# The first unit of an attention stack: its operand stacks sent by two queues in blocks of 128 queries, and two small computations moved behind the first norm

## The chip, the cores and the metric

The kernel runs on one core of one Trainium2 chip. Its engines are TensorE (PE, with its weight loads listed apart as PEld), VectorE (DVE), ScalarE (ACT), GpSimd (POOL) and SyncE (SP); each runs its own instructions in order, and semaphores order them against one another. SP and ACT also issue DMA transfers, each on a queue of its own. The metric is the device time of one launch in microseconds (us), as a median over runs.

## The reference

The input is x, 8 sequences of 512 tokens with 128 features, in float32. Six attention layers run one after another on the normalized input, and a gated feed-forward block closes:

```python
q = (h @ wq.T + bq_).reshape(bh, sl, H, DH)          # H = 16 heads of DH = 8
k = (h @ wk.T + bk_).reshape(bh, sl, H, DH)
scores = jnp.einsum('blhd,bmhd->bhlm', q, k) * inv_sqrt_d
w_avg = jax.nn.softmax(scores, axis=-1).mean(axis=1)
new_w = jax.nn.softmax(CSCALE * w_avg + rel[None], axis=-1)
sa = jnp.einsum('blm,bme->ble', new_w, h)
h1 = _ln(h + sa, l1w, l1b)
h2 = _ln(h1, l2w, l2b)
ff = jax.nn.relu(h2 @ w1.T + b1_) @ w2.T + b2_
return (_ln(h2 + ff, l3w, l3b), None)
```

The heads' softmax weights are averaged over the 16 heads, a fixed decay is added, and a second softmax mixes the rows of h. All 16 x 512 x 512 scores of a sequence must pass through an exponential in each layer. The result is x plus the stack's output, and then that plus the feed-forward block of its norm.

## The kernel before, in words

A unit is one layer of one sequence: 6 layers x 8 sequences = 48 units (`units`, L202), in that order. A unit's scores are made in 16 groups: four blocks of 128 queries (`lc`) times four strips (`turn`) of four heads. A group is four matmuls into PSUM of 128 x 512, for 32 queries and 4 heads each (`scores`, L376): a reduce on DVE takes the negated row maximum (`peak`, L394), ACT takes the exponential and its row sum (`exps`, L399), POOL makes reciprocal weights (`weights`, L406) and PE gathers the weighted sum over heads into `acc` (`gather`, L417). The exponentials of a group stand in a buffer of the pool `e`, which has four; six PSUM buffers (`ring`) hold scores.

The matmul of a strip contracts over 128 partitions that hold four pieces of 32: key and query are each split into a high part (its upper bits) and a low part (the rest), and the products of the parts are stacked. So keys and queries have to be copied into stacks on other partitions before scores can start:

- `norm_in` and `norm_steps` normalize x into h: statistics on DVE, then four POOL instructions.
- `turn_h` transposes h on PE, and ACT copies the result to hT (L223).
- `project_k` and `project_q` multiply hT by the weights, and ACT adds the bias (L230, L239; the query's is the scaled bias `bqs`, made at L148).
- `split` makes the high part on DVE (L247) and the low part on POOL (L248).
- `stack_k` issues 16 DMA transfers of 64 KB on SP's queue (L263): four quarters of the partitions (high, low, high, low) times four strips, the quarter being the outer loop.
- `mask_q` on POOL (L278) spreads a block's queries over four heads with a mask; `stack_q` then issues 16 transfers of 128 KB on SP (L294), eight of the high and eight of the low part. One call of both halves covers two of the four query blocks; blocks 2 and 3 follow during the unit's first steps.

The order is written by hand. Each unit has 32 steps (PAIRS), two score matmuls each. `at(step, place, fn)` puts a function into a table, and the main loop calls what stands there for PE, DVE and ACT after a step's score matmuls, maxima and so on. `place` is the point of the step at which the functions are called, not the engine on which they issue: masks and stacks stand at DVE's place, and issue on POOL and SP. `plan_before` (L501) puts a unit's norm two units ahead of it, its projections, splits and stacks of the first half one unit ahead (steps s+3 to s+21, with s one unit before its own step t), and the second half at t to t+3. `plan_turns` (L488) puts the transposes of the unit after next at the last step of a unit. For units 0 and 1 these steps lie before the first score matmul; steps -64 to -1 are run through with nothing else in them. So the first 40 us hold this chain alone.

Ahead of it stand the loads: two sequences of x, four loads of layer 0 on SP (`load_layer`, L104, with the sum `b2s` of two bias rows on POOL at L118), nine small columns on ACT (L129), and the scaled bias `bqs` on DVE. `b2s` is read only in `affine_b`, during the next unit. `load_layer` is called again during the fifth sequence of each layer for the next one.

Of the kernel before, what the change touches and what calls it, by code (L numbers as in the profile page):

```python
# [9 lines left out]
F32 = mybir.dt.float32  # L10
# [3 lines left out]
ALU = mybir.AluOpType  # L14
# [3 lines left out]
P = 128  # L18
H = 16
STRIPS = 4  # L20
PER_STRIP = H // STRIPS
QB = 32
# [7 lines left out]
def attn_stack_then_ffn(ctx: ExitStack, tc: tile.TileContext, a: dict, out: bass.AP):  # L30
    nc = tc.nc
    ctx.enter_context(tc.manual_schedule())
    x = a["x"]
    B, L, E = x.shape
# [7 lines left out]
    NB = P // QB  # L42
    ISD = 1.0 / math.sqrt(E // H)
# [3 lines left out]
    wts = ctx.enter_context(tc.tile_pool(name="wts", bufs=1))  # L47
    state = ctx.enter_context(tc.tile_pool(name="state", bufs=1))
    proj = ctx.enter_context(tc.tile_pool(name="proj", bufs=2))
    epool = ctx.enter_context(tc.tile_pool(name="e", bufs=4))  # L50
    work = ctx.enter_context(tc.tile_pool(name="work", bufs=2))
# [50 lines left out]
    lay = {}  # L102

    def load_layer(d):  # L104
        qk = wts.tile([P, 2, E], F32, tag="wqk", name=f"wqk_{d}", bufs=2)
        nc.sync.dma_start(qk, a["wqk"][d].rearrange("t e o -> e t o"))
        w1 = wts.tile([P, F], F32, tag="w1", name=f"w1_{d}", bufs=2)
        nc.sync.dma_start(w1, a["w1t"][d])
        w2 = wts.tile([P, FC, E], F32, tag="w2", name=f"w2_{d}", bufs=2)
        nc.sync.dma_start(w2, a["w2t"][d].rearrange("(c p) e -> p c e", p=P))  # L110
        r = wts.tile([P, len(ROWS), E], F32, tag="rows", name=f"rows_{d}", bufs=2)
        nc.sync.dma_start(
            r.rearrange("p k e -> p (k e)"),
            a["rows"][d].rearrange("k e -> (k e)").partition_broadcast(P),
        )
        rows = {name: r[:, k, :] for k, name in enumerate(ROWS)}
        b2s = wts.tile([P, E], F32, tag="b2s", name=f"b2s_{d}", bufs=2)
        nc.gpsimd.tensor_tensor(b2s, rows["ln2_b"], rows["b2"], ALU.add)  # L118
        rows["b2s"] = b2s
        lay[d] = (qk, w1, w2, rows)  # L120

    cols = {}
# [22 lines left out]
        nc.sync.dma_start(fw3s, a["f_w3s"].partition_broadcast(P))  # L145

    bqs = wts.tile([P, D], F32, name="bqs")
    nc.vector.tensor_scalar_mul(bqs, cols["bq_col"], ISD)  # L148


    acc = ps_fix.tile([P, L], F32, name="acc")
# [4 lines left out]
    def ring(shape, n):  # L156
        return ps_big.tile(shape, F32, tag="big", name=n)
# [46 lines left out]
    PAIRS = LC * STRIPS * 2  # L204

    class Unit:
# [50 lines left out]
        def stack_k(self):  # L257


            self.ks = proj.tile([P, STRIPS, L], F32, tag="ks", name=f"ks_{self.n}")  # L260
            for c in range(4):
                for i in range(STRIPS):
                    nc.sync.dma_start(  # L263
                        self.ks[32 * c : 32 * c + 32, i, :],
                        self.kparts[c % 2][32 * i : 32 * i + 32, :],
                    )

        def mask_q(self, two, k, lc):


            key = two, k
            if lc == 2 * two:
                self.stacks[key] = work.tile(
                    [P, 2, NB, PER_STRIP, QB], F32, tag=f"m{k}", name=f"m{k}_{self.n}_{two}", bufs=1
                )
            m = self.stacks[key]
            part = self.qparts[k][:, lc * P : (lc + 1) * P].rearrange("p (n l) -> p n l", l=QB)
            nc.gpsimd.tensor_tensor(  # L278
                m[:, lc - 2 * two],
                part.unsqueeze(2).to_broadcast([P, NB, PER_STRIP, QB]),  # L280
                mask.unsqueeze(1).to_broadcast([P, NB, PER_STRIP, QB]),
                ALU.mult,
            )

        def stack_q(self, two, k):
# [6 lines left out]
            for c in (2 * k, 2 * k + 1):  # L292
                for i in range(STRIPS):
# [2 lines left out]
                        m[32 * i : 32 * i + 32].rearrange("p a n j l -> p (a n j l)"),  # L296
                    )


        def norm_a(self):  # L300
            self.ln = Norm(self.z1, self.z1, f"a{self.n}")
# [159 lines left out]
    PE_, DVE_, ACT_, RING_ = range(4)  # L461
    later = {}

    def at(step, place, fn):
        later.setdefault((step, place), []).append(fn)
# [10 lines left out]
    def matmuls(step, fn):  # L476

        at(step, PE_, lambda: at(step, ACT_, fn()))

    def norm_steps(base, un, make, s0, s1, s2, s3, s4):  # L480

        at(base + s0, DVE_, lambda: (make(), un.ln.stats(0, 2)))
        at(base + s1, DVE_, lambda: un.ln.stats(2, LC))
        at(base + s2, DVE_, lambda: un.ln.aggregate())
        at(base + s3, DVE_, lambda: un.ln.centre())
        at(base + s4, DVE_, lambda: un.ln.scale())

    def plan_turns(u):  # L488


        def run():
            rest = []
            if 0 <= u + 2 < U:
                rest.append(obj[u + 2].turn_h(ring([P, L], f"pt_h{u + 2}")))
            if 0 <= u - 1 < U:
                rest.append(obj[u - 1].turn_u(ring([P, L], f"pt_u{u - 1}")))
            return lambda: [fn() for fn in rest]

        at(u * PAIRS + PAIRS - 1, RING_, run)

    def plan_before(un):  # L501

        t = un.u * PAIRS
        if un.d == 0:
            norm_steps(t - 2 * PAIRS, un, un.norm_in, 9, 14, 26, 28, 29)
        s = t - PAIRS
        matmuls(s + 3, un.project_k)
        matmuls(s + 5, un.project_q)
        at(s + 5, DVE_, un.split_k)
        at(s + 8, DVE_, un.split_q)  # L510
        at(s + 6, DVE_, un.stack_k)
        for k, lc, step in ((0, 0, 18), (0, 1, 19), (1, 0, 20), (1, 1, 21)):
            at(s + step, DVE_, lambda k=k, lc=lc: un.mask_q(0, k, lc))
            at(t + 2 * k + lc, DVE_, lambda k=k, lc=lc: un.mask_q(1, k, 2 + lc))
        for k, step in ((0, 19), (1, 21)):
            at(s + step, DVE_, lambda k=k: un.stack_q(0, k))
            at(t + 2 * k + 1, DVE_, lambda k=k: un.stack_q(1, k))

    def plan_after(un):

        s = (un.u + 1) * PAIRS
        norm_steps(s, un, un.norm_a, 11, 12, 13, 14, 15)
        at(s + 16, DVE_, lambda: un.affine_a(0))
        at(s + 17, DVE_, lambda: un.affine_a(1))
        norm_steps(s, un, un.norm_b, 19, 20, 22, 23, 24)
        at(s + 25, DVE_, lambda: un.affine_b(0))
        at(s + 26, DVE_, lambda: un.affine_b(1))
        s += PAIRS
        for f, step in enumerate((11, 13, 19, 21)):
            matmuls(s + step, lambda f=f: un.hidden(f))  # L530
        for half, step in enumerate((27, 29)):
            at(s + step, PE_, lambda half=half: un.mlp_out(half))
            at(s + step, DVE_, lambda half=half: un.mlp_add(half))
        norm_steps(s, un, un.norm_c, 28, 30, PAIRS, PAIRS + 9, PAIRS + 10)
        at(s + PAIRS + 11, DVE_, lambda: un.affine_c(0))
        at(s + PAIRS + 12, DVE_, lambda: un.affine_c(1))
# [21 lines left out]
    for s in range(-2 * PAIRS, 0):  # L558
        if s % PAIRS == 0:
            u = s // PAIRS + 2  # L560
# [5 lines left out]
    for u, un in enumerate(obj):  # L566
# [12 lines left out]
        for pr in range(PAIRS):  # L579
            s = u * PAIRS + pr  # L580
            lc, turn, half = pr // 8, (pr // 2) % STRIPS, pr % 2
# [11 lines left out]


    plan_turns(U)
    ready = {}
    left = iter(sorted({s for s, _ in later}))
# [135 lines left out]
```

## Time and profile before

| what | value |
|---|---|
| median of 3 runs | 2818.68 us (2818.52 to 2821.95) |
| profiled execution | 2825.2 us, of it the span of the profile 2823.4 us |
| PE busy | 2746.7 us, 97% of the span |
| ACT busy | 2496.5 us, 88% |
| DVE busy | 2393.9 us, 85% |
| POOL busy | 1801.2 us, 64% |
| 3072 score matmuls, their reduces, their exponentials: mean | 477, 682 and 840 ns |
| first score matmul, first exponential | 39.93 and 41.49 us after the span's start |
| first exponential of group 2 | 47.47 us after the start |

The profile is one execution, taken by the hardware profiler. Busy times are sums of the durations of an engine's instructions, which overlap the instructions beside them, so that a mean of 840 ns goes with starts 0.67 us apart. PE's ends are modelled. In a line of the timeline the figures are start, length, engine, line, operation, output and input with their sizes, how many were merged, and in square brackets how long the engine was idle before, and what ended that. SPq and ACTq are the queues on which SP and ACT issue transfers.

### The profile page before, as it was taken

What the parts mean: (1) busy time and instruction counts of PE and PEld (TensorE: products, weight loads), DVE (VectorE), ACT (ScalarE), POOL (GpSimd) and SP (SyncE); (2) the same over time, 40 slices, a digit from 0 to 9 for tenths busy, and PEclk for the clock granted to TensorE, in tenths of its full rate; (3) what the DMA queues carried; (4) which work ended last, traced back from release to release, by engine and by line L of the source; (5) the groups of instructions that cost most, each with busy time, mean ns of one, the idle gap of its engine ahead of it and who ended that gap; (6) DMA issues with size and microseconds to landing.
All of it is one profiled execution on the core that took longest, in us unless ns stands there. A gap on an engine that the chain in (4) does not pass through costs nothing.

```text
span 2823.4 us, 51628 instructions
## 1 busy us (share of the span) xinstructions
PE 2746.7 (97%) x14944; PEld 1370.0 (49%) x14944; DVE 2393.9 (85%) x5942; ACT 2496.5 (88%) x6845; POOL 1801.2 (64%) x2205
## 2 busy tenths in 40 slices
PE   5999999999999999999999999999999999989999
PEld 2444545445454454454544545445445454445554
DVE  4999999999999999999999999999999999921110
ACT  5999999999999999999999999999999999933232
POOL 4668776776766767767677676676776767633210
PEclk9999999999999999999999999999999999999999
DMA  5555444544544445444454454454564444300000
GB/s 117 114 118 132 93 104 104 112 108 106 111 105 107 97 113 115 110 92 103 105 127 104 93 113 106 103 120 94 117 153 95 102 105 110 78 8 8 15 12 8
DMA packets 133387, 271.06 MB, mean 96 GB/s; under 512 B 39024, under 2 KB 56560, under 8 KB 133104
## 3 DMA queue, kind: packets, MB, share of 16 engines
q1 hardware_dynamic: 131808, 267.73, 42.3%
q8 instruction: 119, 1.95, 0.3%
q14 instruction: 164, 1.34, 0.2%
q10 hardware_dynamic: 1296, 0.03, 0.0%
HBM read 13.86 MB, written 2.10 MB: 6 GB/s over the span
## 4 chain that ended last, share of the span: by engine, by line
PE 47%; ACT 22%; DVE 18%; POOL 6%; issue 5%; DMA 0%; SPq 0%; POOLq 0%; ACTq 0%; DVEq 0%
ACT e L399 19%; DVE top L394 14%; PE ps L385 13%; PE acc L420 12%; PE py L348 6%; PE ph L644 6%; PE po L445 3%; PE pk L229 1%; ACT w L427 1%; POOL z L306 1%; PE pq L238 1%; POOL rs_a L178 1%; POOL z L186 1%; POOL z L181 1%; ACT g L338 1%
## 5 line engine op out<-in xcount | busy, mean ns | idle before, releaser
L399 ACT ACTIVATE e<-ps,top 128x512 f32<-128x512 f32 x3072 | 2134.5, 840 | 23.9 <-DVE top L394 20.4
L394 DVE TENSOR_REDUCE top<-ps 128x1 f32<-128x512 f32 x3072 | 1952.5, 682 | 42.9 <-PE ps L385 35.8
L385 PE MATMUL ps<-ks,qs 128*128 128x512 f32 x3072 | 1240.0, 477 | 34.2 <-ACT e L399 26.0
L399 ACT ACTIVATION_READ_ACCUMULATOR e<-ps,top 128x1 f32 x3072 | 1103.5, 359 | 0.0
L385 PEld LDWEIGHTS ps<-ks,qs 128*128 128x128 f32 x3072 | 495.4, 189 | 888.3 <-ACT e L399 661.6
L420 PE MATMUL acc<-e,rp 128*32 128x512 f32 x6144 | 819.1, 605 | 0.8 <-POOL rp L410 0.3
L410 POOL TENSOR_TENSOR rp<-pick,r 128x128 f32<-128x128 f32 x768 | 308.1, 401 | 549.8 <-DVE r L408 265.8
L420 PEld LDWEIGHTS acc<-e,rp 128*32 128x32 f32 x6144 | 121.0, 108 | 263.1 <-issue 126.5
L278 POOL TENSOR_TENSOR m<-hiq,mask 128x512 f32<-128x512 f32 x192 | 245.2, 1277 | 4.8 <-DMA qs<-m 4.8
L278 POOL TENSOR_TENSOR m<-loq,mask 128x512 f32<-128x512 f32 x192 | 245.1, 1277 | 2.6 <-DMA qs<-m 2.6
L445 PEld LDWEIGHTS po<-h,wT 128*128 128x128 f32 x1536 | 201.0, 191 | 18.9 <-DVE wT L437 1.5
L445 PE MATMUL po<-h,wT 128*128 128x129 f32 x1536 | 202.7, 275 | 0.7 <-DVE wT L437 0.7
L336 PE MATMUL pf<-uT,w 128*128 128x512 f32 x384 | 195.8, 591 | 0.0
L348 PEld LDWEIGHTS py<-w,g 128*128 128x128 f32 x1536 | 186.2, 192 | 10.9 <-ACT vT L621 1.1
L348 PE MATMUL py<-w,g 128*128 128x128 f32 x1536 | 186.9, 275 | 0.8 <-ACT vT L621 0.8
L338 ACT ACTIVATE g<-pf,b_col 128x512 f32<-128x512 f32 x192 | 168.2, 876 | 2.2 <-PE pf L336 2.2
L661 DVE TENSOR_TENSOR y<-fo,fw3s 128x512 f32<-128x512 f32 x8 | 5.5, 692 | 175.8 <-PE fo L656 175.8
L427 ACT ACTIVATE w<-acc 128x512 f32<-128x512 f32 x192 | 134.2, 699 | 22.6 <-PE acc L420 22.6
L662 POOL TENSOR_TENSOR y<-y,x_out 128x512 f32<-128x512 f32 x8 | 10.1, 1265 | 199.7 <-DVE y L661 199.7
L408 DVE RECIPROCAL r<-zs 128x4 f32<-128x4 f32 x768 | 130.9, 170 | 5.7 <-ACT e L399 0.3
L437 DVE TENSOR_TENSOR wT<-pt_w,decay 128x512 f32<-128x512 f32 x192 | 126.9, 661 | 4.5 <-PE pt_w L193 4.2
L355 DVE TENSOR_TENSOR z<-py,z 128x256 f32<-128x256 f32 x96 | 40.8, 425 | 105.3 <-PE py L348 105.3
(97 smaller groups left out, 2637.3 us busy)
## 6 DMA issues: line engine op xcount, KB each, us to landing
qs<-m SPq DMA_DIRECT2D x1536, 128.0 KB, 2.4
ks<-hik SPq DMA_DIRECT2D x384, 64.0 KB, 2.0
ks<-lok SPq DMA_DIRECT2D x384, 64.0 KB, 2.0
rows<-in_rows SPq DMA_DIRECT2D x6, 448.0 KB, 5.1
x_in<-in_x SPq DMA_DIRECT2D x8, 256.0 KB, 3.1
x_out<-in_x SPq DMA_DIRECT2D x8, 256.0 KB, 3.1
out<-y SPq DMA_DIRECT2D x8, 256.0 KB, 2.4
w<-in_w1t SPq DMA_DIRECT2D x6, 256.0 KB, 2.9
```

What stands on the lines that cost most here:

```text
L278: nc.gpsimd.tensor_tensor(m[:, lc - 2 * two], part.unsqueeze(2).to_broadcast([P, NB, PER_STRIP, QB]), mask.unsqueeze(1).to_broadcast([P, N ...
L336: nc.tensor.matmul(pf, w1[:, f * P : (f + 1) * P], self.uT, start=True, stop=True)
L338: return lambda: nc.scalar.activation(self.g[:, f, :], pf, AF.Relu, bias=cols["b1_col"][:, k : k + 1])
L348: nc.tensor.matmul(self.py[:, k, :], self.g[:, f, c * P : (c + 1) * P], w2[:, f, :], start=(f == 0), stop=(f == FC - 1),)
L385: nc.tensor.matmul(ps[s], qs[:, nb * P : (nb + 1) * P].bitcast(F32R), un.ks[:, i, :].bitcast(F32R), start=True, stop=True,)
L394: nc.vector.tensor_reduce(top[s], ps[s], AX.X, ALU.max, negate=True)
L399: nc.scalar.activation(self.e[:, nb, :], ps[s], AF.Exp, bias=top[s], accum_out=self.zs[:, nb : nb + 1],)
L410: nc.gpsimd.tensor_tensor(self.rp, pick.unsqueeze(1).to_broadcast([P, NB, QB]), r.unsqueeze(2).to_broadcast([P, NB, QB]), ALU.mult,)
L420: nc.tensor.matmul(acc[nb * QB : (nb + 1) * QB, :], self.rp[:, nb, :], self.e[:, nb, :], start=(self.turn == 0), stop=(self.turn == STRIPS ...
L427: nc.scalar.activation(self.w.rearrange("p c l -> p (c l)"), acc, AF.Exp, scale=1.0 / H)
L445: nc.tensor.matmul(self.po, self.wT[:, c, :], self.unit.h[:, c, 0 : E + 1], start=(c == 0), stop=(c == LC - 1),)
L644: nc.tensor.matmul(ph, wt[:, c, o * P : (o + 1) * P], gg[:, c, :], start=(c == 0), stop=(c == HC - 1),)
```

## The change

- `load_layer` no longer makes `b2s`. A new `sum_rows` makes it on POOL, at step t+3 of the layer's first unit.
- The scaled bias `bqs` is made on DVE at step -32, behind unit 0's norm.
- The transposes of unit 1's h move from step -1, ahead of the first score matmul, to step 1, behind that step's exponentials; the two statistics steps of its norm move from -23 and -18 to -12 and -11.
- For unit 0, `stack_k` sends the low quarters on ACT's queue and the high ones on SP's.
- For unit 0, the stacks of query blocks 0 and 1 are made block by block (`stack_first`): masks of the high and low part of block 0, then 16 transfers of 64 KB, with the strip as outer loop, the low ones on ACT's queue; then the same for block 1, all on SP's. The masks of block 1 stand in two buffers of the pool `e`.
- The other units keep their order; the loops that plan them are only rewritten.

```diff
@@ -114,9 +114,6 @@
             a["rows"][d].rearrange("k e -> (k e)").partition_broadcast(P),
         )
         rows = {name: r[:, k, :] for k, name in enumerate(ROWS)}
-        b2s = wts.tile([P, E], F32, tag="b2s", name=f"b2s_{d}", bufs=2)
-        nc.gpsimd.tensor_tensor(b2s, rows["ln2_b"], rows["b2"], ALU.add)
-        rows["b2s"] = b2s
         lay[d] = (qk, w1, w2, rows)
 
     cols = {}
@@ -145,7 +142,6 @@
         nc.sync.dma_start(fw3s, a["f_w3s"].partition_broadcast(P))
 
     bqs = wts.tile([P, D], F32, name="bqs")
-    nc.vector.tensor_scalar_mul(bqs, cols["bq_col"], ISD)
 
 
     acc = ps_fix.tile([P, L], F32, name="acc")
@@ -260,7 +256,7 @@
             self.ks = proj.tile([P, STRIPS, L], F32, tag="ks", name=f"ks_{self.n}")
             for c in range(4):
                 for i in range(STRIPS):
-                    nc.sync.dma_start(
+                    (nc.scalar if self.u == 0 and c % 2 else nc.sync).dma_start(
                         self.ks[32 * c : 32 * c + 32, i, :],
                         self.kparts[c % 2][32 * i : 32 * i + 32, :],
                     )
@@ -269,7 +265,13 @@
 
 
             key = two, k
-            if lc == 2 * two:
+            if self.u == 0 and two == 0:
+                pool, tag = (work, f"m{k}") if lc == 0 else (epool, "e")
+                self.stacks[key] = pool.tile(
+                    [P, 2, NB, PER_STRIP, QB], F32, tag=tag, name=f"m{k}_first_{lc}",
+                    bufs=1 if lc == 0 else None,
+                )
+            elif lc == 2 * two:
                 self.stacks[key] = work.tile(
                     [P, 2, NB, PER_STRIP, QB], F32, tag=f"m{k}", name=f"m{k}_{self.n}_{two}", bufs=1
                 )
@@ -296,6 +298,25 @@
                         m[32 * i : 32 * i + 32].rearrange("p a n j l -> p (a n j l)"),
                     )
 
+        def stack_first(self, lc):
+
+            if lc == 0:
+                self.stacks[0] = proj.tile([P, STRIPS, 2, NB * P], F32, tag="qs", name="qs_first")
+            for i in range(STRIPS):
+                for c in range(4):
+                    (nc.scalar if c >= 2 and lc == 0 else nc.sync).dma_start(
+                        self.stacks[0][32 * c : 32 * c + 32, i, lc],
+                        self.stacks[0, c // 2][32 * i : 32 * i + 32, lc].rearrange(
+                            "p n j l -> p (n j l)"
+                        ),
+                    )
+
+
+        def sum_rows(self):
+
+            rows = lay[self.d][3]
+            rows["b2s"] = wts.tile([P, E], F32, tag="b2s", name=f"b2s_{self.d}", bufs=2)
+            nc.gpsimd.tensor_tensor(rows["b2s"], rows["ln2_b"], rows["b2"], ALU.add)
 
         def norm_a(self):
             self.ln = Norm(self.z1, self.z1, f"a{self.n}")
@@ -496,25 +517,38 @@
                 rest.append(obj[u - 1].turn_u(ring([P, L], f"pt_u{u - 1}")))
             return lambda: [fn() for fn in rest]
 
-        at(u * PAIRS + PAIRS - 1, RING_, run)
+        at(u * PAIRS + PAIRS - 1 if u != -1 else 1, RING_, run)
 
     def plan_before(un):
 
         t = un.u * PAIRS
         if un.d == 0:
-            norm_steps(t - 2 * PAIRS, un, un.norm_in, 9, 14, 26, 28, 29)
+            first_steps = (20, 21, 26, 28, 29) if un.u == 1 else (9, 14, 26, 28, 29)
+            norm_steps(t - 2 * PAIRS, un, un.norm_in, *first_steps)
+        if un.u == 0:
+            at(-PAIRS, DVE_, lambda: nc.vector.tensor_scalar_mul(bqs, cols["bq_col"], ISD))
         s = t - PAIRS
         matmuls(s + 3, un.project_k)
         matmuls(s + 5, un.project_q)
         at(s + 5, DVE_, un.split_k)
         at(s + 8, DVE_, un.split_q)
         at(s + 6, DVE_, un.stack_k)
-        for k, lc, step in ((0, 0, 18), (0, 1, 19), (1, 0, 20), (1, 1, 21)):
-            at(s + step, DVE_, lambda k=k, lc=lc: un.mask_q(0, k, lc))
-            at(t + 2 * k + lc, DVE_, lambda k=k, lc=lc: un.mask_q(1, k, 2 + lc))
-        for k, step in ((0, 19), (1, 21)):
-            at(s + step, DVE_, lambda k=k: un.stack_q(0, k))
+        for k in range(2):
+            for lc in range(2):
+                at(t + 2 * k + lc, DVE_, lambda k=k, lc=lc: un.mask_q(1, k, 2 + lc))
             at(t + 2 * k + 1, DVE_, lambda k=k: un.stack_q(1, k))
+        if un.b == 0:
+            at(t + 3, DVE_, un.sum_rows)
+        if un.u == 0:
+            for lc in range(2):
+                for k in range(2):
+                    at(s + 18 + lc, DVE_, lambda k=k, lc=lc: un.mask_q(0, k, lc))
+                at(s + 18 + lc, DVE_, lambda lc=lc: un.stack_first(lc))
+            return
+        for k in range(2):
+            for lc in range(2):
+                at(s + 18 + 2 * k + lc, DVE_, lambda k=k, lc=lc: un.mask_q(0, k, lc))
+            at(s + 19 + 2 * k, DVE_, lambda k=k: un.stack_q(0, k))
 
     def plan_after(un):
```

## The prediction

> **What bounds the kernel now.** I read the windows first, to separate the start from the rest. Columns: stretch and length, then busy us of PE, PE weight loads, DVE, ACT and POOL, granted clock, DMA share, GB/s.
>
> ```profile
> 0.00:40.00 40.00, 6.45 (x13) 2.51 (x13) 4.30 (x32) 6.69 (x8) 18.41 (x24) 1.00 0.48 114
> 95.00:2540.00 2445.00, 2410.24 (x13800) 1202.44 (x13793) 2300.60 (x5687) 2355.33 (x6575) 1703.84 (x2093) 1.00 0.47 105
> ```
>
> In the first 40 us no engine is busy for even half the time; afterwards PE and ACT are full. Which of the two paces the long middle is told by ACT's waits between 100 and 2500 us (total, times, longest):
>
> ```profile
> ACT w L427 <- PE acc L420: 22.6, 46, 0.5
> ACT e L399 <- DVE top L394: 12.9, 49, 0.5
> ACT kT L230 <- PE pk L229: 8.6, 42, 0.2
> ```
>
> Of 2400 us ACT waits some 50, never over 0.5 us in attention. ACT runs one exponential after another, about 0.67 us from start to start, while the scores matmul waits 661.6 us on ACT. So a shift of ACT's chain in unit 0 passes to the end one for one, and nothing later absorbs it. What sets the start is in the timeline (start, length, work):
>
> ```profile
> 9.64 0.45 POOL L118 TENSOR_TENSOR b2s<-rows 128x128 f32<-128x128 f32 x1 [7.46 <-DMA rows<-in_rows]
> 9.76 0.36 DVE L148 TENSOR_SCALAR bqs<-bq_col 128x6 f32<-128x6 f32 x1 [7.36 <-DMA bq_col<-in_bq_col]
> 10.03 0.86 DVE L172 BATCH_NORM_STATS2 st_in<-x_in 128x6 f32<-128x128 f32 x4
> ...
> 15.89 0.59 ACT L223 COPY hT<-pt_h 128x512 f32<-128x512 f32 x1 [10.77 <-PE pt_h L193]
> ...
> 19.82 2.49 SPq L263 DMA_DIRECT2D ks<-hik  x4
> ...
> 30.00 10.06 SPq L294 DMA_DIRECT2D qs<-m  x16
> ...
> 39.93 3.85 PE L385 MATMUL ps<-ks,qs 128*128 128x512 f32 x8 [6.51 <-DMA qs<-m]
> ...
> 41.49 0.69 ACT L399 ACTIVATE e<-ps,top 128x512 f32<-128x512 f32 x1 [7.45 <-DVE top L394]
> ```
>
> Two delays follow one another. DVE stands from 2.4 to 9.76 us before the bias scaling, and the first statistics are queued behind it. Then SP issues 32 stack copies, one every 0.63 us, from 19.8 to 40.1 us. The DMA table of the start says what landed when (count, KB, us from issue to landing):
>
> ```profile
> x_in<-in_x SPq DMA_DIRECT2D x2, 256.0 KB, 3.3
> bq_col<-in_bq_col ACTq DMA_DIRECT2D x1, 3.0 KB, 5.6
> ```
>
> The input, issued at 0.74, landed near 4.0 us; the bias, issued at 4.18, at 9.76. A key stack of 64 KB takes as long to issue as a query stack of 128 KB (2.49 us for four of each). During the first the DMA engines were busy 0.46 of the time at 105 GB/s, during the second 0.95 at 210: for the 64 KB copies issue is the limit, not the engines.
>
> **What the Trainium skill says.** "DMA: Bandwidth & Descriptors", section "Issuing engines are not separate DMA queues": copies from several engines share the same 16 DMA engines, and issuing from more than one saves only sequencer time. Here sequencer time is what's short, as the 0.46 shows. "Perfetto Trace Analysis", section "DMA Instruction — HWDGE (DVE, Sync)": the descriptor generator is shared by the issuing sequencers and locked while one uses it. No stretch of this trace has SP and ACT issuing at once, so how much of the 0.63 us is under that lock isn't shown. It is the largest unknown. "TensorE: Matmul & The Clock Gate", section "What's actually happening": an idle PE runs at half rate for about 3.4 us of work. The trace agrees: the key projection took 2.07 us at 16.5 and 1.87 at 43.6, the query projection of the same size 1.13 at 46.3.
>
> **The change, part by part,** in the clock of the profiled execution.
>
> *First norm.* With bias scaling and row sums behind it, the statistics start at about 4.0. From statistics to normalized h took 4.70 us (10.03 to 14.73), to 8.7; the transposes take 1.15, to 9.9. ACT must first finish its nine column loads, the last issued at 9.96 for 0.34: so hT is copied at 10.4 instead of 15.89, −5.5 us. Bounds: −6.0 if ACT were free, −4.5 if the input landed only at 5.5. The scaling (0.36) now waits for 9.76 on DVE, behind the norm; its reader, the query projection, comes at 16.0, so 6 us cover it; uncovered it costs 0.36. The row sum (0.45 on POOL, step 3) waits for rows landed at 9.6; POOL's slack there hides it, otherwise 0.45 late for the next reciprocal weights. In layers 1 to 5 the old place waited 0.1 us in all (7.6 total, 7.5 the first), so moving it is worth nothing.
>
> *Stacks.* With everything 5.5 earlier: split key at 13.9, SP's first stack at 14.3, query projection leaves ACT at 16.7, four masks of 1.24 us each from 18.45 to 23.4, now in the order high and low of block 0, then of block 1. SP sends the eight high key stacks, 14.3 to 19.3. ACT sends the eight low ones from 16.7 to 21.7 if it issues at SP's 0.625, then eight low query stacks of block 0, to 26.7. SP sends the eight high ones from 19.7 to 24.7, and block 1's sixteen to 34.7. The first scores need strip 0: ACT's second query stack, issued at 22.35 and landing 2.0 to 2.4 later, gives 24.45 against 39.93. ACT is the later one for the exponentials: behind its sixteenth issue it starts at 26.75 instead of 41.49, **−14.75 us**. Bounds for ACT's issue: 0.33 us (its small loads) would leave it waiting for scores at about 26.0, 0.7 better; full sharing is rival two. In the built program each queue has only four completion semaphores here, and every copy waits for the fourth before it: four in 2.5 us hold as long as landing stays below 2.5. At 2.6 each of 16 issues takes 0.65: I allow +0.4.
>
> *Second unit's transposes,* moved from ahead of the scores to behind step 1. POOL finishes that unit's norm (3.4 us after the masks) at 26.9, the transposes take 1.1, and the next scores come at 28.1 for exponentials due at 30: hidden by the first four. The copy itself, 0.59 us, now stands in ACT's row: +0.6. The key projection behind it (1.9 cold) ends at 31.95, half a microsecond after ACT wants it: +0.55.
>
> *Borrowed buffers.* Block 1's masks take two of the four buffers of the exponentials. In the built program group 2 therefore reuses group 0's buffer, and its first exponential waits for the gather of group 0. The gather stands on PE behind four scores, the query projection and two scores of group 3: 31.95 + 4×0.48 + 1.1 + 2×0.48 + 1.06 = 37.1. ACT is ready at 34.0: **+3.1 us**. If PE is already warm at 30, the projection is 0.9 shorter and the wait about 2.4. Queued behind that exponential is all of ACT, thus also PE's next scores. Group 3 reuses the buffer of block 1's high mask, whose last copy lands near 34.9, under that wait; group 5 the low mask's, 36.1, far ahead. Group 4 waits for the gather of group 1, which falls within group 3's 2.7 us.
>
> Sum at group 2's first exponential: 47.47 before; −14.75 + 0.6 + 0.55 + 3.1 = −10.4 (to within rounding), with the allowance −10.0. Query blocks 2 and 3 leave SP by 46 and are read near 53, so nothing is late next. The profiled execution took 2825.2 us, 2823.4 of it the span; runs had a median of 2818.68. I take 10.0 off each: span 2813.4, median **2808.7 us**, −0.35%. Under 0.2% (5.6 us) a measurement of this kernel can't tell from no change.
>
> **The rivals.** *One, issue partly shared* (0.15). While both queues issue, each takes 0.75 to 0.95 us; ACT's sixteen end 2 to 5 us later and the gain is 3 to 7.5 us: 2811 to 2816. For it: the shared generator. Against: the engines idle half the time between 64 KB copies.
>
> *Two, issue not parallel at all* (0.09). SP's first four go alone, to 16.8; then the queues alternate, and ACT's sixteenth ends 32 slots later, at 36.8. The first exponential moves by −4.6, hT, the projection and the buffer wait return 4.3: 2818, no change.
>
> *Three, slower* (0.08): ACT held by its own queue. Copies that saturate the engines land late, and each ACT issue waits for the fourth before it. The loads of the first 10 us landed after 5.0 to 6.3 us. At 6.5 us landing ACT issues every 1.62 us, ends at 42.7, and with the 4.3 of ACT and PE waits behind it the time is 2824.3, the bound to slower; 7.5 us gives 2828. Against: query stacks at 0.95 share landed in 2.4.
>
> *Four, the wait for the gather is shorter than thought* (0.02): −12.5 to −14, 2805 to 2806.
>
> **How the numbers follow.** The forecast has 0.66, with −7.5 to −12.5 us: 2806 to 2811. Low 2805, high 2817 leave out rivals two, three and four, 0.19. Faster: 0.66, four, and the better part of one (0.06), 0.74. Same: the rest of one and two, 0.18. Slower: 0.08.
>
> **What would show it.** Statistics starting near 4 us and hT at 10.4: the first part. SP and ACT issues of the same stretch each at 0.62 apart: forecast; 0.75 to 0.95, rival one; above 1.1, two. First scores near 24.5, first exponential near 26.8. An idle stretch of 2 to 3.5 us on ACT ahead of group 2's first exponential, with PE's accumulation (acc) as its end. From group 3 on, every exponential about 10 us earlier than before. It is wrong if ACT's issues take longer than 0.75, if PE stalls for the second unit's h beyond 28, or if the gain at group 3 isn't there at the end.

## The result, and the profile after

| | us |
|---|---|
| before, median of 6 runs (the three shown and three beside the changed kernel) | 2819.74 (2818.52 to 2821.95) |
| changed, median of 6 runs | 2808.64 (2806.88 to 2809.18) |
| ratio, 95% interval | 0.9958 (0.9946 to 0.9971) |
| predicted | 2808.7, from 2805 to 2817 |
| profiled execution after, and its span | 2809.18, 2807.4 |

The change saves 11.1 us of the medians; the prediction said 10.0. That both end at the same 2808.6 or 2808.7 owes something to luck: the before of six runs is 1.1 us above that of the three from which the prediction subtracted.

The windows of the changed kernel come first, in the columns used before (stretch and length, busy us of PE, weight loads, DVE, ACT and POOL, clock, DMA share, GB/s). The last three lines are the stretches in which one queue, then both, send the stacks of unit 0.

```profile
0.00:40.00 40.00, 17.92 (x46) 8.27 (x50) 15.32 (x53) 16.73 (x37) 23.29 (x30) 1.00 0.57 141
95.00:2540.00 2445.00, 2411.74 (x13778) 1204.90 (x13775) 2291.44 (x5679) 2343.22 (x6551) 1709.91 (x2098) 1.00 0.47 104
...
14.90:16.50 1.60, 1.56 (x2) 0.00 (x0) 0.00 (x0) 0.00 (x1) 1.23 (x1) 1.00 0.18 41
16.60:20.00 3.40, 0.00 (x0) 0.00 (x0) 1.48 (x9) 0.58 (x1) 2.28 (x2) 1.00 0.74 171
21.80:26.80 5.00, 2.05 (x4) 1.17 (x4) 1.36 (x3) 0.00 (x0) 4.84 (x6) 1.00 0.88 205
```

PE does 17.9 us of work in the first 40 instead of 6.5, and ACT 16.7 instead of 6.7: 10.0 us of ACT's and 11.5 of PE's work has moved forward. The long middle is what it was. ACT's waits between 100 and 2500 us (total, times, longest) say the same:

```profile
ACT w L448 <- PE acc L441: 23.4, 46, 0.5
ACT e L420 <- DVE top L415: 13.4, 49, 0.5
ACT kT L226 <- PE pk L225: 9.4, 44, 0.2
```

No sum there is more than 0.8 us above that of before, so nothing gave the gain back. The timeline of the start (start, length, work, idle time before it and what ended it) answers to the one that the prediction shows:

```profile
4.27 0.87 DVE L168 BATCH_NORM_STATS2 st_in<-x_in 128x6 f32<-128x128 f32 x4 [1.88 <-DMA x_in<-in_x]
...
10.21 0.17 DVE L529 TENSOR_SCALAR bqs<-bq_col 128x6 f32<-128x6 f32 x1 [4.79 <-DMA bq_col<-in_bq_col]
10.41 0.45 ACTq L126 DMA_DIRECT2D f_h2s_col<-in_f_h2s_col  x1
10.90 0.58 ACT L219 COPY hT<-pt_h 128x512 f32<-128x512 f32 x1 [5.78 <-DMA ln2b_col<-in_ln2b_col]
...
14.82 5.23 SPq L259 DMA_DIRECT2D ks<-hik  x8
...
16.50 0.69 ACT L235 ACTIVATE qT<-pq,bqs 128x512 f32<-128x512 f32 x1 [2.17 <-PE pq L234]
16.56 5.12 ACTq L259 DMA_DIRECT2D ks<-lok  x8
...
20.23 15.12 SPq L307 DMA_DIRECT2D qs_first<-m_first  x24
...
21.77 5.05 ACTq L307 DMA_DIRECT2D qs_first<-m_first  x8
...
24.64 2.05 PE L406 MATMUL ps<-ks,qs_first 128*128 128x512 f32 x4 [8.18 <-DMA qs_first<-m_first]
...
26.87 0.69 ACT L420 ACTIVATE e<-ps,top 128x512 f32<-128x512 f32 x1 [9.69 <-DMA qs_first<-m_first]
...
32.30 0.69 ACT L226 ACTIVATE kT<-pk,bk_col 128x512 f32<-128x512 f32 x1 [0.82 <-PE pk L225]
...
33.55 0.69 ACT L420 ACTIVATE e<-ps,top 128x512 f32<-128x512 f32 x1
...
34.37 0.19 PEld L406 LDWEIGHTS ps<-ks,qs_first 128*128 128x128 f32 x1 [0.36 <-ACT e L420]
34.81 1.07 PE L441 MATMUL acc<-e,rp 128*32 128x512 f32 x8
...
35.99 0.69 ACT L420 ACTIVATE e<-ps,top 128x512 f32<-128x512 f32 x1 [1.67 <-issue]
...
47.65 0.61 ACT L448 ACTIVATE w<-acc 128x512 f32<-128x512 f32 x1
```

The statistics start when the input has landed. The two queues' rows stand side by side, each copy at 0.63 to 0.65 us. The first exponential comes at 26.87, behind ACT's sixteenth issue, instead of 41.49. In front of group 2 (35.99) ACT stands for 1.67 us; the row calls its end "issue", but PE's gather ends at 35.88, 0.11 earlier, and that is taken as the release; the kernel with masks of their own, further down, bears it out. The first mixing exponential of the unit (`w<-acc`) is a mark that all kernels here share. Before, it stood here:

```profile
58.67 0.71 ACT L427 ACTIVATE w<-acc 128x512 f32<-128x512 f32 x1
```

It is 11.0 us earlier now, as the medians have it. (The two profiled spans differ by 16.0. The other 5 us build up by some 0.1 us in each of the 48 units: that one execution of before ran about 0.2% slower throughout, which its other runs don't show.)

### The profile page after: what moved, and what is told of

Its sections match the earlier page's. It is cut to its first block, busy times and chain, and to the rows that moved or that the text cites. A ratio compares the mean times of both kernels' runs of the same rounds, so it can differ in the third digit from the quotient of the medians.

```text
span 2807.4 us, 51664 instructions
## 1 busy us (share of the span) xinstructions
PE 2744.2 (98%) x14944; PEld 1370.9 (49%) x14944; DVE 2391.7 (85%) x5942; ACT 2489.4 (89%) x6845; POOL 1801.3 (64%) x2205
## 4 chain that ended last, share of the span: by engine, by line
PE 44%; ACT 41%; issue 8%; DVE 6%; POOL 1%; SPq 0%; DMA 0%; ACTq 0%; POOLq 0%; DVEq 0%
ACT e L420 35%; PE ps L406 12%; PE acc L441 10%; PE py L369 6%; PE ph L678 6%; DVE top L415 4%; PE po L466 3%; ACT g L359 2%; ACT w L448 2%; PE pk L225 2%; ACT kT L226 1%; PE p L665 1%; PE p L666 1%; PE fo L690 1%; PE pt_w L189 1%
## 5 line engine op out<-in xcount | busy, mean ns | idle before, releaser
L406 PE MATMUL ps<-ks,qs 128*128 128x512 f32 x3040 | 1225.6, 476 | 25.2 <-ACT e L420 17.4
L420 ACT ACTIVATION_READ_ACCUMULATOR e<-ps,top 128x1 f32 x3072 | 1086.6, 354 | 0.0
L406 PEld LDWEIGHTS ps<-ks,qs 128*128 128x128 f32 x3040 | 488.7, 189 | 868.6 <-ACT e L420 637.3
```

Of the source, the lines that this page charges most:

```text
L406: nc.tensor.matmul(ps[s], qs[:, nb * P : (nb + 1) * P].bitcast(F32R), un.ks[:, i, :].bitcast(F32R), start=True, stop=True,)
L420: nc.scalar.activation(self.e[:, nb, :], ps[s], AF.Exp, bias=top[s], accum_out=self.zs[:, nb : nb + 1],)
```

## The experiments

Each kernel is read by three marks: when hT of unit 0 is copied, how long after it the first exponential comes, and how long after it the first mixing exponential. Counting from hT takes out what varies in the loads at the start, from 9.8 to 10.9 us between programs with the same norm.

| kernel | hT | first exponential after hT | mixing after hT | median us (runs), ratio to before, interval |
|---|---|---|---|---|
| before | 15.89 | 25.60 | 42.78 | |
| changed | 10.90 | 15.97 | 36.75 | 2808.64 (6), 0.9958 (0.9946 to 0.9971) |
| norm alone | 9.81 | 25.63 | 42.81 | 2813.34 (18), 0.9980 (0.9973 to 0.9987) |
| norm back | 15.86 | 15.96 | 36.50 | 2813.38 (17), 0.9981 (0.9973 to 0.9988) |
| row sums back | 14.36 | 15.98 | 35.44 | 2811.48 (9), 0.9974 (0.9964 to 0.9984) |
| transposes back | 10.39 | 18.70 | 37.59 | 2809.35 (5), 0.9965 (0.9952 to 0.9978) |
| one queue | 10.42 | 19.67 | 47.94 | 2821.64 (12), 1.0000 (0.9992 to 1.0009) |
| one queue, own masks | 10.75 | 19.66 | 41.57 | 2816.43 (13), 0.9980 (0.9972 to 0.9988) |
| two queues, no blocks | 9.76 | 22.61 | 40.50 | 2813.63 (8), 0.9973 (0.9963 to 0.9983) |
| own masks | 10.39 | 15.99 | 34.50 | 2808.55 (4), 0.9954 (0.9939 to 0.9969) |
| own masks, lean start | 9.87 | 15.20 | 34.01 | 2806.72 (5), 0.9946 (0.9934 to 0.9959) |

The runs were made in three groups, each beside its own runs of before (medians 2821.17, 2819.24 and 2821.76); differences below are to those. The last row is the second run of its kernel.

### The norm's part, alone and taken back

One kernel is the one before with nothing but the bias scaling and the row sums moved:

```diff
...
-        nc.gpsimd.tensor_tensor(b2s, rows["ln2_b"], rows["b2"], ALU.add)
...
-    nc.vector.tensor_scalar_mul(bqs, cols["bq_col"], ISD)
...
+        if un.u == 0:
+            at(-PAIRS, DVE_, lambda: nc.vector.tensor_scalar_mul(bqs, cols["bq_col"], ISD))
+        if un.b == 0:
+            at(t + 3, DVE_, un.sum_rows)
```

> The kernel before, with only the bias scaling and the row sums moved as in the change. Theory (the first norm waited for nothing but these two, and everything up to the first exponential follows it): hT at 10.4 to 10.9 instead of 15.89, first exponential 5.0 to 5.5 earlier (36.0 to 36.5), the time 5.0 to 5.5 under the kernel before. Rival (the stack chain has another wait that takes its place, such as the masks): under 2 us.

It is 5.9 us faster, a little more than expected. The copy of hT moved by 6.1, and both marks after it by the same. Its timeline on ACT:

```profile
9.81 0.59 ACT L219 COPY hT<-pt_h 128x512 f32<-128x512 f32 x1 [4.69 <-DMA f_h1s_col<-in_f_h1s_col]
...
35.44 0.69 ACT L401 ACTIVATE e<-ps,top 128x512 f32<-128x512 f32 x1 [7.47 <-DVE top L396]
```

The other kernel is the changed one with the same lines put back where they were:

> The changed kernel, with the bias scaling and the row sums back in their old places. Theory (the parts add): first exponential 5.0 to 5.5 later than in the changed kernel, near 32, the time 5.0 to 5.5 over it, some 6 us under the kernel before. Rival (the two parts cover one another, since ACT's column loads or the borrowed buffers limit the rest): under 3 us over the changed kernel.

It keeps 5.9 of the 11.1 us; its first exponential is 4.95 later than in the changed kernel, its mixing exponential 4.7. The two parts give 5.9 and 5.9, together 11.8 against 11.1: they add, within what the medians can tell, and neither hides the other. A third puts back the row sums alone:

> The changed kernel, with only the row sums back in their old place on POOL. Theory (POOL's part of the norm stands behind the sum, which waits for the rows to land at 9.6 to 10): POOL's first norm instruction at 10.1 instead of 5.51, hT at 14.7 instead of 10.90, the time 3.8 us over the changed kernel. Rival (only the bias scaling was in the way): no difference.

It is 7.8 us faster than before, so it loses 3.3 of the change's 11.1. POOL's timeline shows how, with an operation of 0.45 us:

```profile
9.31 0.45 POOL L118 TENSOR_TENSOR b2s<-rows 128x128 f32<-128x128 f32 x1 [7.14 <-DMA rows<-in_rows]
9.72 0.20 POOL L176 TENSOR_TENSOR rs_in<-mv_in,eps 128x4 f32<-128x4 f32 x1
```

POOL waits 7.1 us for the rows, and the norm's reciprocal is queued behind it: 9.72 instead of 5.51. So moving the scaling alone gives only part of the gain: POOL becomes the place where the norm waits. Of the 3.46 us at hT only 2.15 are left at the mixing exponential. In this run PE took 1.25 us for the second unit's key projection instead of 2.08, and ACT's 0.82 ahead of kT were gone, which is 0.8 of the missing 1.3. The small wait that the changed kernel has at group 5 (0.25) is gone too. The medians, 3.3 us apart, are too uncertain to confirm this return.

### The stacks: one queue

The changed kernel with all of unit 0's stacks on SP:

```diff
-                    (nc.scalar if self.u == 0 and c % 2 else nc.sync).dma_start(
+                    nc.sync.dma_start(
...
-                    (nc.scalar if c >= 2 and lc == 0 else nc.sync).dma_start(
+                    nc.sync.dma_start(
```

> The changed kernel, with all of unit 0's stacks on SP's queue (block order, masks and norm as changed). Theory (both queues issue at full rate, and ACT's chain sets the end): SP needs 16 issues of 0.64 us for keys and 16 for block 0, first exponential near 30.4 instead of 26.87; block 1's high mask is read until 45.2, so group 3 starts 6.0 later than in the changed kernel (45.2 instead of 39.22), and the time is 2814.3, about 5.7 over the changed kernel. Rival (two queues share what they need, and the block order alone brings the gain): at most 1 us later at group 3, 2809.6 or less. Rival (the second queue halves all issue, 10 us): 9 us later, near 2818.

The first exponential came where it was expected, 3.7 us later than with two queues when counted from hT. But the whole gain was gone, where 5.7 us of it had been expected to go: 2821.64 beside 2821.17. Its timelines show where, POOL's masks first, then PE's gathers and ACT's exponentials:

```profile
34.98 2.50 POOL L280 TENSOR_TENSOR m<-hiq,mask 128x512 f32<-128x512 f32 x2 [8.20 <-DMA qs_first<-m_first]
...
39.29 1.84 PE L441 MATMUL acc<-e,rp 128*32 128x512 f32 x8 [2.09 <-POOL rp L431]
45.37 1.94 PE L441 MATMUL acc<-e,rp 128*32 128x512 f32 x8
50.99 1.94 PE L441 MATMUL acc<-e,rp 128*32 128x512 f32 x8
...
41.23 0.69 ACT L420 ACTIVATE e<-ps,top 128x512 f32<-128x512 f32 x1 [4.58 <-issue]
...
47.42 0.69 ACT L420 ACTIVATE e<-ps,top 128x512 f32<-128x512 f32 x1 [2.83 <-issue]
...
53.04 0.69 ACT L420 ACTIVATE e<-ps,top 128x512 f32<-128x512 f32 x1 [2.83 <-issue]
```

Three stalls, 10.2 us. In the built program the two borrowed buffers come back only for groups 5 and 6 (the trace doesn't name the buffers). Groups 2, 3 and 4 then share the two other buffers, and each waits for the gather of the group two before it, which ends 0.1 us ahead of it. The first gather itself waits 2.09 us for POOL's weights, and POOL is in turn held by masks whose buffer SP's copies still read: 8.20 us in the row above. There is one more part, the clock that PE was granted. Its window (columns as before):

```profile
39.50:53.00 13.50, 11.10 (x32) 2.71 (x24) 6.26 (x13) 6.16 (x17) 5.03 (x7) 0.50 0.71 158
```

PE ran at half its clock while ACT stalled, and a gather took 1.84 to 1.94 us instead of 1.07. By my estimate from these rows, the gathers alone make some 2.5 of the 10.2 us. To tell the second queue from the borrowed buffers, one more kernel has one queue and no borrowing (the edit of the masks is shown further down):

> All of unit 0's stacks on SP's queue, block 1's masks in a buffer of their own. Theory (the run with one queue gave back 10.7 us at group 5 instead of 5.7 because groups 2, 3 and 4 had to alternate between two buffers): none of the three gaps of ACT (4.58, 2.83, 2.83 us) is there, the first exponential stays near 30.1, the first block's mixing exponential comes near 48.6 instead of 58.4, and the time is some 10 us under the run with one queue, 1.5 over the changed kernel. What is left against the run with own masks and two queues, 3.7 us, is what the second queue is worth by itself. Rival (POOL's late reciprocal weights or the late stacks of block 1 hold the groups anyway): gaps of the same sum, less than 3 us under the run with one queue.

Each against its own runs of before, it is 5.8 us faster than one queue with borrowed buffers, little more than half of what I expected, and the three old stalls are gone. New ones took their place, from its timelines on SP, PE, DVE and ACT:

```profile
24.86 20.20 SPq L313 DMA_DIRECT2D qs_first<-m_first  x32
...
39.62 1.38 PE L447 MATMUL acc<-e,rp 128*32 128x512 f32 x8 [2.09 <-POOL rp L437]
...
42.48 0.69 ACT L426 ACTIVATE e<-ps,top 128x512 f32<-128x512 f32 x1 [0.91 <-DVE top L421]
...
45.10 0.58 SPq L97 DMA_DIRECT2D x_in<-in_x  x1
...
48.49 0.49 DVE L168 BATCH_NORM_STATS2 st_in<-x_in 128x6 f32<-128x128 f32 x2 [2.32 <-DMA x_in<-in_x]
48.89 2.46 DVE L421 TENSOR_REDUCE top<-ps 128x1 f32<-128x512 f32 x4
...
49.66 0.69 ACT L426 ACTIVATE e<-ps,top 128x512 f32<-128x512 f32 x1 [2.69 <-DVE top L421]
```

The input of unit 2 is issued at 45.10, behind 32 copies, instead of 35.40 in the changed kernel. DVE's statistics wait 2.32 us for it, the maxima behind them are late, and ACT stands 2.69 us. The 0.91 before it is the rival's cause: the first gather again waits 2.09 us for POOL's weights, the scores queued behind it are late, and so are their maxima. So the second queue is worth 7.1 us at the mixing exponential (41.57 against 34.50 from hT): 3.7 at the first exponential, and 3.4 because SP's other work, the next input above all, and POOL's masks aren't held back.

### The stacks: two queues without the blocks

Here the 64 KB copies by block of 128 queries become again the 128 KB copies of both blocks, the low ones sent by ACT, with no borrowed buffers:

```diff
-            if self.u == 0 and two == 0:
+            if False:
...
-                    nc.sync.dma_start(
+                    (nc.scalar if self.u == 0 and two == 0 and k else nc.sync).dma_start(
...
```

> The changed kernel with two queues, but unit 0's query stacks made as before: masks of both blocks first, then eight transfers of 128 KB on SP (high) and eight on ACT (low); no borrowed buffers. Theory (64 KB transfers on two queues just fit into the DMA engines, 128 KB transfers don't): the two streams share some 220 GB/s while both run, ACT's last issue ends near 31 to 32, first exponential near 32 (26.87 in the changed kernel), no wait of group 2 for a gather, time about 3.8 us over the changed kernel, 2812.4. Rival (issue is the only limit, the engines carry both): ACT issues every 0.63 us, first exponential near 30.4, 1.4 us over, 2810.0. Rival (block order is worth nothing, since the borrowed buffers give it back): equal or faster than the changed kernel.

The time came as expected: 7.5 us faster than before, thus 3.6 us of the change's gain lost. So did the first exponential, at 32.37, but with hT 1.1 earlier than in the changed kernel. Counted from hT it is 6.6 later than with blocks, and 2.9 of it comes back, most of that since the buffer waits are gone and kT waits 0.18 instead of 0.82. Beside the kernel with own masks (below), which doesn't borrow either, the blocks are worth 6.0 us at the mixing exponential (34.50 against 40.50 from hT). The DMA table of its start (KB each, us from issue to landing):

```profile
qs<-m SPq DMA_DIRECT2D x24, 128.0 KB, 2.5
...
qs<-m ACTq DMA_DIRECT2D x8, 128.0 KB, 4.4
```

and the window in which both queues send them (the columns as before), with ACT's row of the timeline:

```profile
22.80:26.40 3.60, 0.00 (x0) 0.00 (x0) 0.00 (x0) 0.00 (x0) 3.17 (x4) 1.00 1.01 213
...
22.77 6.70 ACTq L296 DMA_DIRECT2D qs<-m  x8
```

This is in part rival three's mechanism: the engines are full, landing grows to 4.4 us, and ACT's eight issues take 6.70 us, 0.84 each instead of 0.63. It costs 1.7 us here, not the 10 and more that the rival needed. Waiting for the fourth copy before is 0.7 of it: the trace has ACT's seventh issue at 27.85 and the third, of 24.08, landing after 3.7 us; likewise the eighth at 28.96 and the fourth, of 24.73, after 4.2. The rest is issues that themselves took up to 1.05 us while the engines were full.

### The second unit's transposes put back

```diff
-        at(u * PAIRS + PAIRS - 1 if u != -1 else 1, RING_, run)
+        at(u * PAIRS + PAIRS - 1, RING_, run)
```

> The changed kernel, with unit 1's transposes back ahead of the first score matmul. Theory (the second unit's h is ready only near 27, after the first scores could start): PE waits for it, first scores near 28.4 instead of 24.64, first exponential near 30.0 instead of 26.87; the hT copy (0.6) and the wait for the key projection (0.8) leave ACT's row, so the time is 1.7 us over the changed kernel. Rival (where they stand is worth nothing): within 0.5 us.

```profile
26.79 1.12 PE L189 MATMUL pt_h<-ident,h 128*128 128x128 f32 x4 [10.84 <-POOL h L182]
27.55 3.83 PE L406 MATMUL ps<-ks,qs_first 128*128 128x512 f32 x8
...
27.94 0.59 ACT L219 COPY hT<-pt_h 128x512 f32<-128x512 f32 x1 [11.26 <-DMA qs_first<-m_first]
29.09 0.69 ACT L420 ACTIVATE e<-ps,top 128x512 f32<-128x512 f32 x1 [0.57 <-DVE top L415]
```

PE waits with the first scores for the second unit's h and the first exponential is 2.7 us late. Two thirds of that return, 1.3 us of them because the copy of hT is done before the exponentials begin and the key projection no longer comes too late. 0.84 us are left at the mixing exponential, half the expected 1.7. The medians (9.9 faster than before, against 11.1) agree, but by themselves couldn't tell this from the changed kernel.

### Masks with a buffer of their own

Block 1's masks are given the space of a tile (tag "g") that isn't used so early, in place of two buffers of the exponentials:

```diff
-                pool, tag = (work, f"m{k}") if lc == 0 else (epool, "e")
...
+                    if k == 0:
+                        self.pair = work.tile([P, FC, L], F32, tag="g", name="m_first_1", bufs=1)
+                    self.stacks[key] = self.pair[:, 2 * k : 2 * k + 2, :].rearrange(
...
```

> The changed kernel with block 1's masks in the buffer of the feed-forward's hidden layer, which is free then, instead of two buffers of the exponentials. Theory (group 2 waits for the gather of group 0 only because it has to reuse its buffer): the 1.67 us gap of ACT before group 2 goes, and the gaps of 0.25 to 0.35 before group 5, so everything from the second block on is 2.0 us earlier: 2806.6. Rival (scores or maxima are late there too, and take the wait's place): gap stays over 1 us, 2808 to 2808.6.

From hT the mixing exponential is 2.25 us earlier: ACT has no wait left at group 2, which gives 1.8, nor at group 5, which gives the rest. Against its own runs of before it gains 12.6, the changed kernel 11.1 against its own; the intervals overlap, so that 2.25 is shown by the trace, and by the medians only as a tendency.

A last version adds three things to it: four columns that only the last part needs are loaded later and by SP, ACT sends six low query stacks instead of eight, and kT of unit 1 is taken up by ACT one step later.

```diff
-        nc.scalar.dma_start(cols[name], a[name])
+        if not name.startswith("f_"):
+            nc.scalar.dma_start(cols[name], a[name])
...
-                    (nc.scalar if c >= 2 and lc == 0 else nc.sync).dma_start(
+                    (nc.scalar if c >= 2 and lc == 0 and i < 3 else nc.sync).dma_start(
...
+        if un.u == 1:
+            at(s + 3, PE_, lambda: at(s + 4, ACT_, un.project_k()))
```

> The changed kernel with block 1's masks in a buffer of their own, and three further waits of ACT's chain taken away: the four columns of the last feed-forward are loaded later, on SP (hT of unit 0 then waits for its transposes only, 10.2 instead of 10.90); ACT sends two query stacks fewer, SP two more (first exponential 0.75 earlier); unit 1's key bias is added one step later, when the projection is there (0.8). Theory (each is on ACT's chain, so they add): 2.0 + 0.7 + 0.75 + 0.8, 4.2 us under the changed kernel, 2804.4. Rival (the chain has another limit close behind, such as masks or strip 0's landing): at most 2.5 under, 2806 or more.

That gave 2807.6 us in four runs, 13.6 below its before: against the 11.1 of the changed kernel some 2.5 more, where 4.2 had been expected. I ran it again beside the changed kernel on one chip:

> The leaner start once more, beside the changed kernel on the same chip. Theory (its trace had the first block's mixing exponential 4.0 us before the changed kernel's, and held that at later units): 3.5 to 4.2 us under the changed kernel. Rival (the 4 us of the trace are chance of two executions): within 1.5 us of it.

> The changed kernel itself, beside the leaner start on the same chip. Theory: some 11 us under the kernel before, first exponential within 0.7 us of 26.87, the gap of ACT before group 2 again near 1.7 us, since it is set by the order on PE and not by chance.

The changed kernel gave 2810.0 (0.9958 again, 0.9945 to 0.9970), the lean version 2806.72: 15.0 us below before and 3.3 below the changed kernel, just under the range expected. The gap of the changed kernel at group 2 was 1.84 us this time. The mark on ACT, of the changed kernel in this run and then of the lean one:

```profile
46.97 0.61 ACT L448 ACTIVATE w<-acc 128x512 f32<-128x512 f32 x1
```

```profile
43.88 0.61 ACT L457 ACTIVATE w<-acc 128x512 f32<-128x512 f32 x1
```

3.1 us earlier, and all of it is at the end. Beside own masks only 0.5 of the last three edits' gain is left at this mark (34.01 against 34.50 from hT). At group 2 it was still 1.2, but SP now sends two more copies, and the next input is late again. From the lean version's timelines on SP, DVE and ACT:

```profile
35.60 0.58 SPq L97 DMA_DIRECT2D x_in<-in_x  x1
...
40.04 0.49 DVE L171 BATCH_NORM_STATS2 st_in<-x_in 128x6 f32<-128x128 f32 x2 [0.59 <-DMA x_in<-in_x]
...
41.21 0.69 ACT L429 ACTIVATE e<-ps,top 128x512 f32<-128x512 f32 x1 [0.43 <-DVE top L424]
```

Even so this version is the fastest of the kernels here.

## Why the prediction was right, step by step

**What bounds the kernel.** A shift of ACT's chain in unit 0 was to pass to the end one for one. It did: in every run of the table the shift of the mixing exponential from before and that of the median agree within 1.2 us, and in the first run of the lean version within 1.5. (The 661.6 us quoted for the scores matmul stand in the row of its weight loads.)

**First norm.** Predicted −5.5 at hT, measured −5.0 in the changed kernel and −6.1 with the norm's part alone; the bounds were −4.5 and −6. ACT's last column load is the end of the wait, as the step had it. (The 0.34 us given for that load belong to the one before it; in the trace of before it took 0.45, and 10.4 fits that.) That load was issued at 10.41 instead of 9.96, and the start differs by such amounts from run to run: the changed kernel, run again, copied hT at 10.16.

**First scores and first exponential.** Predicted 24.45 and 26.75, measured 24.64 and 26.87. Two errors cancel in that: hT was 0.5 late, but ACT's queue began to issue at 16.56, 0.06 after its last activation had begun, where the step let it begin only after the 0.69 of that activation. The sixteen issues took 10.26 us, 0.26 over sixteen times 0.625; the allowance was 0.4.

**Issue in parallel.** This was the largest unknown, and rivals one (0.75 to 0.95 us each) and two (above 1.1) hung on it. SP's 24 copies took 0.63 each, ACT's sixteen 0.64, in the same stretch, and SP alone had needed 0.63. The lock on the shared generator that the Trainium skill names ("Perfetto Trace Analysis", "DMA Instruction — HWDGE (DVE, Sync)"; it speaks of DVE and Sync, here it is ACT and SP) thus costs nothing that can be seen at two issues per 0.63 us. "DMA: Bandwidth & Descriptors", "Issuing engines are not separate DMA queues", calls the time saved by issuing from several engines usually small relative to the DMA itself; here the measurement decides, and it is worth 3.7 us at the first exponential and 7.1 in all; 64 KB copies went from 105 to 171 and 205 GB/s.

**Second unit's transposes and key projection.** Predicted 0.6 for the copy and 0.55 for the wait. The copy at 29.54 moved the next exponential by 0.46, and kT waited 0.82 for a projection that ran cold, 2.08 us. Together 1.28 against 1.15. How much of it runs cold differs from program to program: the traces' record of the granted clock begins, at full, only 32.90 us into the changed kernel, behind this projection (30.18 to 32.26). With the transposes back it begins at 32.15, within the projection (1.50 us), and with the row sums back at 33.93, early in it (1.25 us).

**Borrowed buffers.** This is the term that was mis-sized: 3.1 us predicted, 1.67 measured. The step added the busy times of PE's queue, key projection, scores, query projection, scores, gather, to 37.1 (written out, the sum makes 37.0; the total below it makes −10.5, not −10.4). That is wrong twice. Rows of overlapping matmuls can't be added: the query projection is charged 1.02 us, but the scores behind it start 0.45 after it (33.40 and 33.85). And PE wasn't the bound at all: the last scores ahead of the gather wait until ACT's last exponential of group 1 (33.55 to 34.24) frees their PSUM buffer. From there it is nearly fixed: 0.13 to the weight load at 34.37, 0.44 to the gather, 1.07 of gather, 0.11 to ACT. So the wait doesn't depend on how fast PE's projections were. In the kernels with the norm back, with the row sums back and with the transposes back it is 1.67 us too, though PE's key projection took from 1.25 to 1.82 us in them; in the second run of the changed kernel it is 1.84. The fallback that the step named, 2.4 us if PE was warm, was off for the same reason, and so was the sign that was announced, 2 to 3.5 us of idle ACT. That the wait comes from the borrowed buffer is shown by the kernel with own masks, which has none there.

**Sum.** At group 2's first exponential −10.0 predicted, −11.48 measured: 1.43 of that is the buffer wait. A small wait at group 5 (0.25), which the step thought far ahead, and slightly later starts before it take 0.5 back; −11.0 is left at the mixing exponential. So the forecast of −10.0 is 1.1 short of the medians' −11.1, and would be further off without these later losses. What the working did not foresee is PE's clock. The same stretch in the changed kernel and in the one with own masks (columns as before):

```profile
39.80:43.10 3.30, 3.30 (x12) 1.36 (x12) 1.81 (x4) 3.30 (x11) 1.52 (x2) 0.50 1.01 205
```

```profile
39.80:43.10 3.30, 3.11 (x17) 1.17 (x21) 3.30 (x8) 3.30 (x11) 1.06 (x2) 1.00 1.04 212
```

Behind the buffer wait the changed kernel's PE was granted half its clock, and its next gather took 1.93 us; where masks had their own buffer the clock stayed full and group 5 didn't wait. The row sums back and the transposes back had the buffer wait without the drop, so what sets it off isn't shown.

**"Nothing is late next."** SP's stacks ended at 46.2, the step said 46, and nothing was late. But the sentence rests on the second queue: with one queue SP's next input was 10 us later and cost 2.69 us on ACT; in the lean version two more copies on SP cost 0.43. The working did not look at that load.

**Edits costed at nothing.** The bias scaling behind the norm ran at 10.21, 6 us ahead of its reader; the row sums ran at 33.12 on POOL. Neither shows as a releaser of a wait on ACT. The move of the second unit's statistics was not tried alone; they stand some 0.35 us behind the query's split in both traces (22.56 behind 22.21 before, 17.56 behind 17.22 after). Rival three's slower issue appeared only with 128 KB copies on both queues, and there cost 1.7 us. Its premise that the first loads landed after 5.0 to 6.3 us holds for part of them: ACT's columns before landed after 1.7 to 5.6.

## What to carry to other kernels

If copies are small enough that issuing them takes longer than moving them, a second issuing queue can send as many again in the same time, as long as the DMA engines are half idle, and the first queue's later loads gain by it too; count what stands behind the copies on each queue. Before a buffer wait is priced, ask whether the engine that must release it is itself paced by the waiting engine: then the wait is a short tail behind that engine's last step, and not a sum of busy times. And look at the clock where an engine stalls: a PE that is granted half of it lengthens the next wait. A slow start of an engine's chain is worth its full length where everything after it runs back to back, and an operation of 0.4 us that waits for a late load costs what the load costs, to all that is queued behind it.

## What the runs showed of the hardware

Two queues issuing SBUF to SBUF copies of 64 KB at once didn't slow each other (0.63 and 0.64 us each), at up to 205 GB/s and a share of 0.88. With 128 KB copies on both, the engines were full at 213 GB/s and ACT's copies landed after 4.4 us instead of 2.4. Late landing alone didn't slow the issue: behind the input's 256 KB, SP by itself sent sixteen 128 KB copies that landed after 3.8 us (changed kernel, 36.08 to 46.19), one every 0.63 us.

PE's clock can fall in such a start: it was granted 0.50 from 39.8 to 43.1 us in the changed kernel, and from 39.5 to 53.0 with one queue, where gathers took up to 1.94 us instead of 1.07.

The first stretch of a program is less repeatable than the rest: the copy of hT came between 9.8 and 10.9 us in programs with the same norm, and the second unit's key projection took 2.08, 1.5 or 1.25 us, as the full clock came behind it, within it or early in it.
